# Attention and octonion feed-forward on one Trainium2 core: down weights expanded on GpSimd, one deviation for the second sequence's layer norm, gate products begun among the last scores, longer lags in the planner

## The chip, the core and the metric

The kernel runs on one NeuronCore of one Trainium2 chip. The time is that of the device, in microseconds, for one execution of the whole program, and the runs of the kernel before have a median of 1032.09 us. The core has a matrix engine (TensorE, PE in the profile; its weight loads are PEld), three other compute engines (VectorE or DVE, ScalarE or ACT, GpSimd or POOL), and a queue engine for transfers (SyncE or SP). Each runs its own list of instructions in order, and an instruction waits until the semaphores of what it needs have been raised. DMAs are issued from the lists of SP and POOL.

## The reference

The input x has 2 sequences of 1024 tokens of 512 values. Everything is float32.

```python
xn = (x - mean(x)) / sqrt(var(x) + eps)                      # per token
q, k, v = split(xn @ w_qkv.T + b_qkv)                        # 32 heads of 16
scores = q @ k.T / 4 + slope[head] * position[key]           # ALiBi, causal
s = (softmax(scores) @ v) @ w_out.T + b_out
Wq = clip(round(W / mean|W|), -1, 1) * mean|W|               # ternary weights
gate, up = oct(xn, w_gate), oct(xn, w_up)                    # 512 -> 1360
ffn = oct(silu(gate) * up, w_down)                           # 1360 -> 512
out = x + s * silu(ffn)
```

An `oct` layer treats its features as 8 components. Its full matrix consists of the 8 component matrices, each used 8 times with a sign from the octonion multiplication table. "Expanding" a weight means writing these signed copies out.

## The kernel before, in words

**Tiling.** Tokens lie on 16 tiles of 128. Attention is cut into 32 units (b, g, qc): a sequence, one of 8 groups of 4 heads, and one half of the queries (512 columns). Each unit is worked twice. The first pass makes scores (L566) only to find a maximum for each query: DVE reduces the banks (tiles `s` and `s_d`, written into `left` and `mx`), and `split_max` and `place_max` (L619, L631; small products `pm`) put the maxima into two rows of the query stack `q_stack`, with small GpSimd DMAs from `mr`. The second pass makes the scores with the maximum already subtracted (L682), adds the causal mask by a product (L701), ACT takes the exponential into `p` (128x512 at a time), and `p` times the values accumulates in `po` (L720), with the sums of the exponentials in extra rows.

**A unit's result.** `finish` (L733) yields six chores: `sums` fetches the sums with a DMA into `l`, `invert` takes the reciprocal on DVE, `keep` stores it to DRAM (`ld`), `spread` (L757) loads it into `r`, each head's row repeated on 32 partitions, `divide` (L765) multiplies `po`'s copy by `r` on DVE, and `store` writes the result to `att`, from which the output projection loads `oT` (products `pout`, L803). Each chore has a lag in ns, which the planner lets pass before it writes the next one.

**Side work among the scores.** Projections to queries and keys (`pqk`, L479), values (`pv`, L439), transposes of the normed tokens (`ptx`, L404) and the output projection are placed among the score products. So are the weights of the feed-forward part. For `w_down`, `expand_down` (L354) writes the signed copies for each of four parts kp into one buffer `m_d` with 8 activations on ACT, in two halves, and `turn_down` (L366) transposes them on PE (tile `ptd`), copies them with ACT to `md`, and stores them to DRAM (`mw`) with GpSimd DMAs. The buffer of `m_d` is single. `md` is in the ring of tag "ot", which has two buffers and also holds `r`.

**Second sequence.** Tokens 8 to 15 are normed during the score phase, by `more_tokens` (L975), in two groups of four: load four tiles, `measure` on DVE, `deviation` (a square root on ACT, which needs another function table than the exponential) and `factors`, `normal` on ACT, and the transposes.

**Order.** Until `held.clear()` (L1392) all compute and DMA-issuing instructions keep the order in which the Python code emits them on each engine (`InOrder`, L59). That order is written by a planner (L1107 to L1390) which counts its own time `now` and, for every engine, a time when it would be free (`run_pe`, `run_act`, `run_dve`). At each `step` it takes the next ready score product, or else value products, the small products for the maxima, and side work by due time (`next_side`, `next_behind`). `later` puts items in the list `behind` with a position at which they may begin and a model of their cost. `do_chores` emits the chores of finished units, `try_fill` the loads of `q_stack` and `k_stack`.

**Gate phase.** After the loop, the normed tokens are split into a part in the reduced format and a remainder (`split`, L1410: GpSimd makes `xh`, DVE makes `xl`). `expand_in` (L1429) writes gate and up weights of a 128-row tile from their signs, gate on ACT and up on DVE. `gate_up` (L1447) makes 8 products each for `pg` and `pu` (L1455), and `down` (L1476) accumulates the down projection (`pd`, L1497). The work goes over 4 blocks of 512 tokens and 11 hidden tiles. The last chunks of the output projection stand among them.

Of the kernel before, what the change touches and what calls it, by code (L numbers as in the profile page):

```python
# [10 lines left out]
F32 = mybir.dt.float32  # L11
# [7 lines left out]
P = 128  # L19
# [56 lines left out]
def kernel(  # L76
# [277 lines left out]
    def expand_down(kp, half):  # L354

        if half == 0:
            nat[kp] = wop.tile([P, 8, H8], F32, tag="wo", name=f"m_d_{kp}")
        for k in range(4 * half, 4 * half + 4):
            act_.activation(
                nat[kp][:, k, :],  # L360
                w_tiles["d"][:, k ^ kp * 2, :],
                AF.Identity,
                scale=sgn["d"][:, kp, k : k + 1],
            )

    def turn_down(kp, first):  # L366

        m = nat[kp].rearrange("p k o -> p (k o)")
        last = min(first + 4, NM)
        pt = ps_m.tile([P, 4, P], F32, tag="m", name=f"ptd_{kp}_{first}")  # L370
        for mt in range(first, last):
            fs = min(P, HID - mt * P)
            pe(nc.tensor.transpose(pt[:fs, mt - first, :], m[:, mt * P : mt * P + fs], ident))
        md = wk.tile([P, 4, P], F32R, tag="ot", name=f"md_{kp}_{first}")
        full = min(last, HID // P) - first
        act_.copy(md[:, 0:full, :], pt[:, 0:full, :])
        pool_.dma_start(
            out=mw[first : first + full, :, kp, :].rearrange("m p n -> p m n"),
            in_=md[:, 0:full, :].bitcast(F32),
        )  # L380
        if last == NM:
            fs = HID - (NM - 1) * P
            act_.copy(md[:fs, full, :], pt[:fs, full, :])
            pool_.dma_start(out=mw[NM - 1, 0:fs, kp, :], in_=md[:fs, full, :].bitcast(F32))
# [348 lines left out]
    def finish(b, g, qc):  # L733


        posb = po_tiles.pop((b, g, qc))
        key = f"{b}_{g}_{qc}"
        box = {}

        def sums():  # L740
            box["l"] = wk.tile([P, 16], F32, tag="l", name=f"l_{key}", bufs=1)
            sp_.dma_start(
                out=box["l"],
                in_=posb[HD:P:32, :].rearrange("h (a n) -> h a n", n=16),
            )

        def invert():
            box["rl"] = wk.tile([P, 16], F32, tag="rl", name=f"rl_{key}", bufs=1)
            dve_.reciprocal(box["rl"], box["l"])

        def keep():
            box["dram"] = spill.tile([4, 512], F32, tag="l", name=f"ld_{key}")
            sp_.dma_start(
                out=box["dram"].rearrange("h (a n) -> (h a) n", n=16), in_=box["rl"]
            )

        def spread():  # L757
            box["r"] = wk.tile([P, 512], F32, tag="ot", name=f"r_{key}")
            for h in range(4):
                sp_.dma_start(  # L760
                    out=box["r"][32 * h : 32 * h + 32],
                    in_=box["dram"][h : h + 1].to_broadcast([32, 512]),
                )

        def divide():  # L765
            dve_.tensor_tensor(box["r"], posb, box["r"], ALU.mult)

        def store():
            sp_.dma_start(out=att[b, g, :, qc * 512 : qc * 512 + 512], in_=box["r"])


        return [
            (sums, 0, 9000),
            (invert, 250, 300),
            (keep, 0, 3500),
            (spread, 0, 7000),
            (divide, 620, 300),
            (store, 0, 4500),
        ]

# [124 lines left out]
        return "weights" not in known  # L905

    def waits_x():
        return any(it[2] == "x" or it[2] and it[2][0] == "n" for it in behind)


    order = sorted(range(len(side)), key=lambda n: side[n][0])
# [55 lines left out]
    def spread(kp, half):  # L967
        later(
            lambda: expand_down(kp, half),
            lambda: set_known(  # L970
                ("e", kp), run_act(max(now[0], known["w", "d"]), 1300)
            ),
        )

    def more_tokens(t0):  # L975

        for t in range(t0, t0 + 4):
            later(
                lambda t=t: measure(t, 4),
                lambda t=t: set_known(("m", t), run_dve(max(now[0], known["x"]), 900)),  # L980
                "x",
            )
            begin[0] += 0.2
        later(
            lambda: (deviation(t0, 4), factors(t0, 4)),
            lambda: run_dve(run_act(known["m", t0 + 3], 2800), 350),
        )
        for t in range(t0, t0 + 4):
            begin[0] += 0.3
            later(  # L990
                lambda t=t: normal(t, 4),
                lambda t=t: set_known(("n", t), run_act(now[0], 720)),
            )
            later(lambda t=t: norm_item(t), None, ("n", t), 436, "t")

    def load_wo():
        wo_sb.append(wop.tile([P, KD, D], F32, tag="wo", name="wo_sb"))
# [94 lines left out]
        for f in range(0, NM, 4):  # L1092
            later(lambda kp=kp, f=f: turn_down(kp, f), None, ("e", kp), 436, "t")
    later(lambda: set_known("weights", 0))
    for t0 in (8, 12):
        begin[0] = 3 if t0 == 8 else 5.4
        later(
            lambda t0=t0: [load_x(t, sp_) for t in range(t0, t0 + 4)],
            lambda: set_known("x", now[0] + 9000),
        )  # L1100
        begin[0] += 0.4
        more_tokens(t0)
    begin[0] = 10
    later(load_wo)
    side = [(d, ok or (lambda: True), it) for d, ok, it in lead_in + side]
# [14 lines left out]
    RUN = 1800  # L1120
    HELD = 1e12
    now, kind = [HEAD], ["F"]
    act, dve = [0.0], [0.0]
    e_free, x_free, m_free = [0.0] * 2, [0.0] * 3, [0.0] * 2
    o_free = [0.0]
    p_ready, placed, fill_at = {}, {}, []
# [12 lines left out]
    def run_act(t, cost):  # L1139
        act[0] = max(act[0], t) + cost  # L1140
        return act[0]

    def run_dve(t, cost):
        dve[0] = max(dve[0], t) + cost
# [195 lines left out]
    def step():  # L1340
# [10 lines left out]
        if kind[0] == "R" and soon(scores):  # L1351
            scores[0][3]()
            return True
        rest = next_value() + next_turn() + next_side(pos) + next_behind(pos)
        rest.sort(key=lambda f: (max(f[0], now[0] + SOON), f[1]))
        if soon(rest) and (left[0] > 0 or not soon(scores)):
            left[0] -= rest[0][2]
# [20 lines left out]
            for m in range(2):  # L1378
                sp_.dma_start(out=swapped[:, :, m, :], in_=pairs[:, :, 1 - m, :])

    left = [RUN]
    while E[0] < len(exps) or V[0] < len(vals) or S_[0] < len(side) or behind:
        try_fill()
        do_chores()
        try_fetch()
        if not w_again and unit_of(exps, E[0]) >= NU - 5:
            fetch_signs()
        if not step():
            now[0] += 500
            assert now[0] < 1e8  # L1390

    held.clear()  # L1392


    fw = []
    for t in [
        k_ring[2],
        k_ring[3],
        k_ring[4],
        q_ring[3],  # L1400
        k_ring[1],
        q_ring[2],
        k_ring[0],
        vp.tile([P, 4, 3 * P], F32R, tag="v", name="fw_7"),
    ] + [pp.tile([P, 4, 512], F32R, tag="p", name=f"fw_{n}") for n in (8, 9, 10)]:
        t = t.rearrange("p h n -> p (h n)")[:, 0 : 12 * P]
        fw.append(t.rearrange("p (s n) -> p s n", n=P))
    halves, downs = {}, {}

    def split(tb):  # L1410
# [11 lines left out]
        dve_.tensor_tensor(xl, src, xh, ALU.subtract)  # L1422
        halves[tb] = (xh, xl)

    def load_fw(mt):
        fs = min(P, HID - mt * P)
        sp_.dma_start(out=fw[mt][:fs, 8:12, :].bitcast(F32), in_=mw[mt, 0:fs])

    def expand_in(mt):  # L1429

        fs = min(P, HID - mt * P)
        for n in range(2):
            for kt in range(KD):
                f = 0
                while f < fs:
                    k, o = divmod(mt * P + f, H8)
                    size = min(fs - f, H8 - o)
                    dst = fw[mt][:, 4 * n + kt, f : f + size]
                    src = w_again[n][:, k ^ kt * 2, o : o + size]
                    sign = sgn["i"][:, kt, k : k + 1]  # L1440
                    if n:
                        dve_.tensor_scalar_mul(dst, src, sign)
                    else:
                        act_.activation(dst, src, AF.Identity, scale=sign)
                    f += size

    def gate_up(tb, mt):  # L1447
        fs = min(P, HID - mt * P)
        pg = ps_x.tile([P, 512], F32, tag="x0", name=f"pg_{tb}_{mt}")
        pu = ps_x.tile([P, 512], F32, tag="x1", name=f"pu_{tb}_{mt}")  # L1450
        for n0, ps in ((0, pg), (4, pu)):
            for kt in range(KD):
                for n, part in enumerate(halves[tb]):
                    pe(
                        nc.tensor.matmul(  # L1455
                            ps[:fs, :],
                            lhsT=fw[mt][:, n0 + kt, 0:fs],
                            rhs=part[:, kt, :],
                            start=(kt == 0 and n == 0),
                            stop=(kt == KD - 1 and n == 1),  # L1460
                        )
                    )
        sg = wk.tile([P, 512], F32, tag="oT", name=f"sg_{tb}_{mt}")
        act_.activation(sg[:fs, :], pg[:fs, :], AF.Silu, scale=scale["g"][:fs, 0:1])
        h = wk.tile([P, 512], F32, tag="y", name=f"h_{tb}_{mt}")
# [78 lines left out]

    s_tiles = []
    fetch_last()
    split(0)
    for mt in range(2):
        expand_in(mt)
    for mt in range(NM):  # L1550
        load_fw(mt)

# [99 lines left out]
```

## Time and profile before

| | value |
|---|---|
| runs of the kernel before | 1032.09 us median (1031.54 to 1032.76) |
| profiled execution, its own time | 1030.97 us |
| its span | 1029.1 us |
| mean granted TensorE clock | 0.991 |
| PE busy | 988.5 us (96%) |
| DVE busy | 581.4 us (56%) |
| ACT busy | 490.6 us (48%) |
| POOL busy | 171.7 us (17%) |
| exponentials 128x512 | 576 at 596 ns |
| hardware queue of SP | 74384 packets, 111.40 MB, 35.1% of 16 engines |

The profile comes from one execution. Its page lists busy times, the granted clock, the DMA queues and the costliest groups of instructions; the trace behind it can be asked for the waits of an engine, for the busy time in stretches of the span, and for single instructions. A line such as "engine op out<-in shapes xcount | busy, mean" is a group of instructions, "L" is the line in the kernel (L69 is the helper that passes on every instruction except those of PE, so those are told apart by tile names). In a wait, the arrow names what ended it. In a line of the timeline, the first number is the start in us from the beginning of the span, the second the duration, and the brackets hold the idle time of the engine just before, with its releaser. DVE, ACT, POOL and SP being idle costs nothing by itself.

### The profile page before, as it was taken

How to read it: one execution, taken by the hardware profiler on the slowest of the kernel's cores; microseconds unless marked ns; L12 is line 12 of the kernel's file. 1: busy time of each engine (PE TensorE's matmuls, PEld its weight loads, DVE VectorE, ACT ScalarE, POOL GpSimd, SP SyncE). 2: the span in 40 equal slices, each digit the busy share in tenths (PEclk: the TensorE clock that was granted, in tenths of full speed). 3: DMA queues.
4: the chain of work that ended last, by engine and by line, in shares of the span. 5: the costliest groups of instructions: out<-in, count | busy, mean ns of one | idle time of the engine just before them, and what ended most of it. 6: DMA issues, size and time to landing. Idle time of an engine off the chain costs nothing. (4 is left out here: it accounts for less than half of the span.)

```text
span 1029.1 us, 15486 instructions
## 1 busy us (share of the span) xinstructions
PE 988.5 (96%) x5290; PEld 669.1 (65%) x5290; DVE 581.4 (56%) x1726; ACT 490.6 (48%) x942; POOL 171.7 (17%) x289
## 2 busy tenths in 40 slices
PE   8999988999999999899999999989999999999996
PEld 6655645775666676656667656545476678788784
DVE  6588945776577675676766757748251132231312
ACT  4034456756656554456654556556761132232322
POOL 7701023100200200010010000010021133232322
PEclk9999998999999999999999999999999999999998
DMA  5854735244454423433533244532242113030201
GB/s 203 244 150 154 169 129 167 63 131 154 144 150 138 137 66 123 152 109 117 166 95 96 84 130 148 124 100 79 86 148 82 51 66 109 1 123 1 94 29 42
DMA packets 77935, 117.16 MB, mean 114 GB/s; under 512 B 19624, under 2 KB 29488, under 8 KB 77856
## 3 DMA queue, kind: packets, MB, share of 16 engines
q1 hardware_dynamic: 74384, 111.40, 35.1%
q0 software_dynamic: 3424, 4.64, 1.6%
q8 instruction: 42, 0.69, 0.3%
q14 instruction: 37, 0.30, 0.1%
q10 hardware_dynamic: 48, 0.13, 0.0%
HBM read 77.77 MB, written 37.56 MB: 112 GB/s over the span
## 5 line engine op out<-in xcount | busy, mean ns | idle before, releaser
L69 ACT ACTIVATE p<-s 128x512 f32<-128x512 f32 x576 | 319.4, 596 | 183.4 <-PE s L701 105.7
L682 PE MATMUL s<-q_stack,k_stack 128*128 128x512 f32 (+3 forms) x768 | 263.0, 408 | 4.9 <-ACT p L69 4.5
L69 DVE TENSOR_REDUCE left<-s 128x1 f32<-128x512 f32 x256 | 161.4, 681 | 71.2 <-PE s L566 70.9
L682 PEld LDWEIGHTS s<-q_stack,k_stack 128*128 128x128 f32 x768 | 132.4, 191 | 88.3 <-ACT p L69 44.2
L69 DVE CUSTOM_DVE_ANT_0 nowhere<-s_d,mask 128x384 uint8<-128x384 f32 (+2 forms) x384 | 139.6, 419 | 21.4 <-PE s_d L566 20.0
L720 PE MATMUL po<-p,v 128*32 128x512 f32 (+3 forms) x1536 | 142.6, 491 | 2.8 <-ACT p L69 2.8
L566 PE MATMUL s_d<-k_stack,q_stack 126*128 126x384 f32 (+3 forms) x512 | 128.5, 348 | 4.0 <-DVE mx L69 3.6
L479 PE MATMUL pqk<-xnT,wq 128*128 128x512 f32 x256 | 128.3, 601 | 3.2 <-ACT md L69 1.2
L69 POOL DMA_DIRECT2D q_stack<-mr x64 | 31.0, 488 | 558.5 <-ACT mr L69 558.5
L69 DVE SCALAR_TENSOR_TENSOR h<-pu,sc_u,sg 128x512 f32<-128x512 f32 (+1 forms) x44 | 33.0, 750 | 152.2 <-PE pu L1455 146.7
L566 PEld LDWEIGHTS s_d<-k_stack,q_stack 126*128 126x128 f32 x512 | 83.4, 192 | 26.4 <-DVE mx L69 11.2
L69 DVE CUSTOM_DVE_ANT_0 s_d<-s_d,mask 128x512 f32<-128x512 f32 x128 | 85.6, 715 | 21.9 <-PE s_d L566 21.6
L566 PE MATMUL s<-k_stack,q_stack 126*128 126x512 f32 x256 | 86.5, 422 | 7.9 <-DMA q_stack<-sp 5.7
L69 POOL TENSOR_TENSOR hs<-h,hs 128x512 fp32r<-128x512 f32 (+1 forms) x43 | 56.2, 1307 | 211.6 <-ACT hs L69 211.6
L720 PEld LDWEIGHTS po<-p,v 128*32 128x32 f32 x1536 | 43.4, 109 | 72.6 <-issue 57.9
L701 PE MATMUL s<-mask_r,ident_r 128*128 128x256 f32 (+1 forms) x320 | 89.7, 280 | 0.0
L69 ACT ACTIVATE sg<-pg,sc_g 128x512 f32<-128x512 f32 (+1 forms) x44 | 30.2, 687 | 104.4 <-PE pg L1455 104.4
L69 ACT CAST hs<-h 128x512 fp32r<-128x512 f32 (+1 forms) x44 | 27.3, 620 | 84.4 <-DVE h L69 84.4
L439 PE MATMUL pv<-wv,xnT 128*128 128x256 f32 x256 | 65.1, 384 | 0.0
L701 PEld LDWEIGHTS s<-mask_r,ident_r 128*128 128x128 f32 x320 | 61.1, 191 | 2.8 <-issue 1.7
L566 PEld LDWEIGHTS s<-k_stack,q_stack 126*128 126x128 f32 x256 | 47.1, 190 | 23.6 <-issue 5.8
L479 PEld LDWEIGHTS pqk<-xnT,wq 128*128 128x128 f32 x256 | 44.5, 190 | 27.2 <-issue 18.6
(149 smaller groups left out, 1152.0 us busy)
## 6 DMA issues: line engine op xcount, KB each, us to landing
sp<-st SPq DMA_DIRECT2D x32, 512.0 KB
k_stack<-sp SPq DMA_DIRECT2D x128, 128.0 KB
q_stack<-sp SPq DMA_DIRECT2D x128, 128.0 KB
wqr<-in_wqk_dram SPq DMA_DIRECT2D x16, 512.0 KB
r<-ld SPq DMA_DIRECT2D x128, 64.0 KB
att<-r SPq DMA_DIRECT2D x32, 256.0 KB
xt<-in_x_dram SPq DMA_DIRECT2D x16, 256.0 KB
oT<-att SPq DMA_DIRECT2D x32, 128.0 KB
```

The source lines that it names most:

```text
L69: ins = issue(*args, **kwargs)
L439: nc.tensor.matmul(ps[:, 0:256], lhsT=xnT[:, c, b * S + kt * P : b * S + (kt + 1) * P], rhs=wv_tiles[2 * b + hh][:, c, :], start=(c == 0), ...
L479: nc.tensor.matmul(ps, lhsT=wq_tiles[b, gp][:, kt, which, :], rhs=xnT[:, kt, b * S + c * 512 : b * S + (c + 1) * 512], start=(kt == 0), st ...
L566: nc.tensor.matmul(ps, lhsT=q_of(b, g, qc)[0 : NR - 2, h, tl * P : (tl + 1) * P], rhs=k_of(b, g, c)[0 : NR - 2, h, :n], start=True, stop=True,
L682: nc.tensor.matmul(ps[:, c0 : c0 + w], lhsT=k_of(b, g, kt // 4)[0:NR, h, kt % 4 * P : (kt % 4 + 1) * P], rhs=q[0:NR, h, 512 - w : 512], st ...
L701: pe(nc.tensor.matmul(out, lhsT=ident_r, rhs=rhs, start=False, stop=True))
L720: nc.tensor.matmul(po[32 * i : 32 * i + 32, 512 - w : 512], lhsT=v[:, kt, h * VC : h * VC + 32], rhs=p[:, i * part + c0 : i * part + c0 + ...
```

## The change

The diff does five things.

1. `expand_down` runs on GpSimd instead of ACT (32 multiplies of 128x170), and the planner counts a time for GpSimd (`gps`, `run_pool`). `md` moves from the ring "ot" to the ring "oT".
2. `spread` issues one DMA instead of four, whose source repeats each of the 4 rows 32 times. The lags after `invert`, `spread` and `divide` grow from 300 to 2000, 7000 to 8000 and 300 to 2500 ns.
3. For the second sequence, all eight token tiles are measured first; there is one `deviation` and one `factors`. Tokens 12 to 15 are normed next, then tokens 8 to 11 are loaded a second time and normed. `waits_x` covers the three loads.
4. When the exponentials have reached the last unit but one and all maxima are placed, `try_ahead` splits the first block and expands gate and up weights of hidden tiles 0 and 1, on GpSimd and DVE. It then offers 24 gate and up products of the first block (`pg_0`, `pu_0` and `pg_1`, the last in the bank "x2") to the planner through `next_ahead`. What is not taken is emitted after the loop.
5. As a result of 4, `expand_in`, `split` and the buffers `fw` move ahead of the loop, and `gate_up` uses the products that have been begun.

The number of instructions on PE is the same. ACT has 898 instead of 945 instructions, POOL 335 instead of 291, SP 606 instead of 698.

```diff
     def expand_down(kp, half):
...
-            act_.activation(
-                nat[kp][:, k, :],
-                w_tiles["d"][:, k ^ kp * 2, :],
-                AF.Identity,
-                scale=sgn["d"][:, kp, k : k + 1],
+            pool_.tensor_scalar_mul(
+                nat[kp][:, k, :], w_tiles["d"][:, k ^ kp * 2, :], sgn["d"][:, kp, k : k + 1]
             )
...
-        md = wk.tile([P, 4, P], F32R, tag="ot", name=f"md_{kp}_{first}")
+        md = wk.tile([P, 4, P], F32R, tag="oT", name=f"md_{kp}_{first}")
...
         def spread():
             box["r"] = wk.tile([P, 512], F32, tag="ot", name=f"r_{key}")
-            for h in range(4):
-                sp_.dma_start(
-                    out=box["r"][32 * h : 32 * h + 32],
-                    in_=box["dram"][h : h + 1].to_broadcast([32, 512]),
-                )
+            sp_.dma_start(
+                out=box["r"],
+                in_=box["dram"].rearrange("h (e n) -> h e n", e=1).to_broadcast([4, 32, 512]),
+            )
...
             (sums, 0, 9000),
-            (invert, 250, 300),
+            (invert, 250, 2000),
             (keep, 0, 3500),
-            (spread, 0, 7000),
-            (divide, 620, 300),
+            (spread, 0, 8000),
+            (divide, 620, 2500),
             (store, 0, 4500),
...
     def waits_x():
-        return any(it[2] == "x" or it[2] and it[2][0] == "n" for it in behind)
+        return any(it[2] and it[2][0] in "xn" for it in behind)
...
             lambda: set_known(
-                ("e", kp), run_act(max(now[0], known["w", "d"]), 1300)
+                ("e", kp), run_pool(max(now[0], known["w", "d"]), 1500)
             ),
...
+    def more_tokens():
+
+        begin[0] = 3
+        load_tokens(8, "x")
+        begin[0] += 0.4
+        measure_tokens(8, "x")
+        load_tokens(12, "x2")
+        begin[0] += 0.4
+        measure_tokens(12, "x2")
+        later(
+            lambda: (deviation(8, 8), factors(8, 8)),
+            lambda: run_dve(run_act(now[0], 2800), 350),
+            ("m", 15),
+        )
+        normal_tokens(12, "x2")
+        load_tokens(8, "x3")
+        begin[0] += 0.4
+        normal_tokens(8, "x3")
...
-        rest = next_value() + next_turn() + next_side(pos) + next_behind(pos)
+        rest = next_value() + next_turn() + next_side(pos) + next_behind(pos) + next_ahead()
...
-    def expand_in(mt):
+    def expand_in(mt, parts=(0, 1), beside=False):
...
-                    if n:
-                        dve_.tensor_scalar_mul(dst, src, sign)
+                    if n or beside:
+                        eng = pool_ if beside and n != mt else dve_
+                        eng.tensor_scalar_mul(dst, src, sign)
                     else:
                         act_.activation(dst, src, AF.Identity, scale=sign)
...
+    def try_ahead():
+        if ahead_at[0] < HELD or M[0] < len(maxs) or len(placed) < NU:
+            return
+        if unit_of(exps, E[0]) < NU - 2:
+            return
+        expand_in(0, (0,), True)
+        split(0)
+        expand_in(0, (1,), True)
+        expand_in(1, (0, 1), True)
+        ahead_at[0] = run_dve(now[0], 6500)
+        run_dve(now[0], 2500)
+        for mt, n in ((0, 0), (0, 1), (1, 0)):
+            begun[mt, n], products = gate_or_up(0, mt, n)
+            ahead.extend(products)
+
+    def next_ahead():
+        if not ahead:
+            return []
+
+        def go():
+            ahead.pop(0)()
+            run_pe("R", ready, 227)
+
+        ready = ahead_at[0]
+        return [(ready, 8, 0, go)]
...
-    split(0)
-    for mt in range(2):
-        expand_in(mt)
+    while ahead:
+        ahead.pop(0)()
     for mt in range(NM):
         load_fw(mt)
```

More of the change, by code (lines that the diff above doesn't have):

```diff
@@ L970, in spread, with load_tokens, measure_tokens, normal_tokens @@
             lambda: set_known(
-                ("e", kp), run_act(max(now[0], known["w", "d"]), 1300)
+                ("e", kp), run_pool(max(now[0], known["w", "d"]), 1500)
             ),
         )
-    def more_tokens(t0):
+    def load_tokens(t0, key):
+        later(
+            lambda: [load_x(t, sp_) for t in range(t0, t0 + 4)],
+            lambda: set_known(key, now[0] + 9000),
+        )
+    def measure_tokens(t0, key):
         for t in range(t0, t0 + 4):
             later(
-                lambda t=t: measure(t, 4),
-                lambda t=t: set_known(("m", t), run_dve(max(now[0], known["x"]), 900)),
-                "x",
+                lambda t=t: measure(t, 8),
+                lambda t=t: set_known(("m", t), run_dve(max(now[0], known[key]), 900)),
+                key,
             )
             begin[0] += 0.2
[L984 to L987, printed above, removed]
+    def normal_tokens(t0, key):
         for t in range(t0, t0 + 4):
@@ L990, in more_tokens @@
             later(
-                lambda t=t: normal(t, 4),
-                lambda t=t: set_known(("n", t), run_act(now[0], 720)),
+                lambda t=t: normal(t, 8),
+                lambda t=t: set_known(("n", t), run_act(max(now[0], known[key]), 720)),
+                key,
             )
             later(lambda t=t: norm_item(t), None, ("n", t), 436, "t")
+    def more_tokens():
[6 more added lines that the diff above has]
+        measure_tokens(12, "x2")
+        later(
+            lambda: (deviation(8, 8), factors(8, 8)),
+            lambda: run_dve(run_act(now[0], 2800), 350),
+            ("m", 15),
+        )
+        normal_tokens(12, "x2")
+        load_tokens(8, "x3")
+        begin[0] += 0.4
+        normal_tokens(8, "x3")
     def load_wo():
@@ L1094 @@
     later(lambda: set_known("weights", 0))
[L1095 to L1102, printed above, removed]
+    more_tokens()
     begin[0] = 10
@@ L1122 @@
     now, kind = [HEAD], ["F"]
-    act, dve = [0.0], [0.0]
+    act, dve, gps = [0.0], [0.0], [0.0]
     e_free, x_free, m_free = [0.0] * 2, [0.0] * 3, [0.0] * 2
@@ L1141, in run_act, with run_pool @@
         return act[0]
+    def run_pool(t, cost):
+        gps[0] = max(gps[0], t) + cost
+        return gps[0]
     def run_dve(t, cost):
@@ L1379, in fetch_signs, with add_fw @@
                 sp_.dma_start(out=swapped[:, :, m, :], in_=pairs[:, :, 1 - m, :])
[L1381 to L1392, printed above, removed]
-    fw = []
[L1396 to L1405, printed above, removed]
+    fw = []
+    def add_fw(t):
         t = t.rearrange("p h n -> p (h n)")[:, 0 : 12 * P]
         fw.append(t.rearrange("p (s n) -> p s n", n=P))
+    for t in (k_ring[2], k_ring[3], k_ring[4], q_ring[3], k_ring[1], q_ring[2], k_ring[0]):
+        add_fw(t)
     halves, downs = {}, {}
@@ L1423, in split @@
         halves[tb] = (xh, xl)
-    def load_fw(mt):
+    def expand_in(mt, parts=(0, 1), beside=False):
         fs = min(P, HID - mt * P)
-        sp_.dma_start(out=fw[mt][:fs, 8:12, :].bitcast(F32), in_=mw[mt, 0:fs])
-    def expand_in(mt):
-        fs = min(P, HID - mt * P)
-        for n in range(2):
+        for n in parts:
             for kt in range(KD):
@@ L1445, in expand_in, with gate_or_up, product @@
                     f += size
+    def gate_or_up(tb, mt, n):
+        fs = min(P, HID - mt * P)
+        tag, name = (("x0", "pg"), ("x1", "pu"))[n] if (tb, mt) != (0, 1) or n else ("x2", "pg")
+        ps = ps_x.tile([P, 512], F32, tag=tag, name=f"{name}_{tb}_{mt}")
+        def product(kt, i):
+            pe(
+                nc.tensor.matmul(
+                    ps[:fs, :],
+                    lhsT=fw[mt][:, 4 * n + kt, 0:fs],
+                    rhs=halves[tb][i][:, kt, :],
+                    start=(kt == 0 and i == 0),
+                    stop=(kt == KD - 1 and i == 1),
+                )
+            )
+        return ps, [lambda kt=kt, i=i: product(kt, i) for kt in range(KD) for i in range(2)]
@@ new lines @@
+    ahead, ahead_at, begun = [], [HELD], {}
+    def try_ahead():
[12 more added lines that the diff above has]
+            ahead.extend(products)
@@ new lines, in next_ahead @@
+    def next_ahead():
[6 more added lines that the diff above has]
+        return [(ready, 8, 0, go)]
+    left = [RUN]
+    while E[0] < len(exps) or V[0] < len(vals) or S_[0] < len(side) or behind:
+        try_fill()
+        do_chores()
+        try_fetch()
+        if not w_again and unit_of(exps, E[0]) >= NU - 5:
+            fetch_signs()
+        try_ahead()
+        if not step():
+            now[0] += 500
+            assert now[0] < 1e8
@@ L1447, in gate_up, with load_fw @@
+    held.clear()
+    for t in [vp.tile([P, 4, 3 * P], F32R, tag="v", name="fw_7")] + [
+        pp.tile([P, 4, 512], F32R, tag="p", name=f"fw_{n}") for n in (8, 9, 10)
+    ]:
+        add_fw(t)
+    def load_fw(mt):
+        fs = min(P, HID - mt * P)
+        sp_.dma_start(out=fw[mt][:fs, 8:12, :].bitcast(F32), in_=mw[mt, 0:fs])
     def gate_up(tb, mt):
         fs = min(P, HID - mt * P)
-        pg = ps_x.tile([P, 512], F32, tag="x0", name=f"pg_{tb}_{mt}")
-        pu = ps_x.tile([P, 512], F32, tag="x1", name=f"pu_{tb}_{mt}")
@@ L1451, in gate_up @@
[L1451 to L1462, printed above, removed]
+        both = []
@@ L1463, in gate_up @@
+        for n in range(2):
+            if tb == 0 and (mt, n) in begun:
+                ps = begun.pop((mt, n))
+            else:
+                ps, products = gate_or_up(tb, mt, n)
+                for emit in products:
+                    emit()
+            both.append(ps)
+        pg, pu = both
         sg = wk.tile([P, 512], F32, tag="oT", name=f"sg_{tb}_{mt}")
```

## The prediction

> **What bounds the kernel now.** I read the page's busy shares first, then the windows of the stages that the diff touches, then TensorE's waits, then the timeline at each wait. The shares say who sets the time:
>
> ```profile
> PE 988.5 (96%) x5290; PEld 669.1 (65%) x5290; DVE 581.4 (56%) x1726; ACT 490.6 (48%) x942; POOL 171.7 (17%) x289
> ```
>
> TensorE (PE) is busy for 988.5 of 1029.1 us. The change takes no product away from it, so only its 40.6 us of idle time, and time in which it runs at a lower clock, can be won. The windows (columns PE, PEld, DVE, ACT, POOL, then the granted clock, DMA share and GB/s) show where that lies:
>
> ```profile
> 120.00:150.00 30.00, 24.79 (x101) 13.15 (x93) 17.98 (x34) 15.57 (x38) 6.29 (x10) 0.94 0.45 140
> 150.00:180.00 30.00, 25.23 (x142) 16.71 (x142) 16.60 (x72) 18.52 (x46) 9.98 (x22) 0.89 0.49 155
> 180.00:240.00 60.00, 60.00 (x374) 42.37 (x373) 42.52 (x129) 38.50 (x69) 4.84 (x7) 1.00 0.34 104
> 718.00:750.00 32.00, 30.49 (x180) 15.41 (x181) 9.02 (x39) 23.80 (x61) 0.96 (x2) 1.00 0.30 99
> ```
>
> From 120 to 180 us, where the down weights are expanded and turned, PE is idle for 10.0 of 60 us and its clock falls; from 180 us on it is never idle, at 1.00. The seam to the gate phase (718 to 750) loses 1.5 us by the window. PE's waits (total, times, longest) name the rest:
>
> ```profile
> PE s L566 <- DMA q_stack<-sp: 5.7, 3, 3.4
> PE s L682 <- ACT p L69: 4.5, 7, 1.5
> PE s_d L566 <- DVE mx L69: 3.6, 5, 2.7
> PE po L720 <- ACT p L69: 2.8, 2, 2.2
> PE s L566 <- DVE left L69: 2.2, 1, 2.2
> ```
>
> The timeline says what is late behind these names (start, duration, then in brackets the idle time before and its releaser). First the 120 to 180 stage:
>
> ```profile
> 136.53 0.58 ACT L69 CAST md<-ptd 128x512 fp32r<-128x512 f32 x1 [3.28 <-DMA mw<-md]
> 137.17 0.70 PE L479 MATMUL pqk<-xnT,wq 128*128 128x512 f32 x1 [1.20 <-ACT md L69]
> 155.76 0.50 PE L682 MATMUL s<-q_stack,k_stack 128*128 128x512 f32 x1 [1.46 <-ACT p L69]
> 166.49 0.62 PE L720 MATMUL po<-p,v 128*32 128x512 f32 x1 [2.21 <-ACT p L69]
> ```
>
> ACT, in its written order, stands 3.28 us at a copy whose buffer is not yet stored; exps queue behind it, and PE waits for those exps or for the bank. Then the divisions and one fill:
>
> ```profile
> 95.11 0.69 DVE L69 TENSOR_TENSOR r<-posb,r 128x512 f32<-128x512 f32 x1 [2.73 <-DMA r<-ld]
> 96.46 0.50 PE L566 MATMUL s<-k_stack,q_stack 126*128 126x512 f32 x1 [2.20 <-DVE left L69]
> 423.49 0.69 DVE L69 TENSOR_TENSOR r<-posb,r 128x512 f32<-128x512 f32 x1 [4.13 <-DMA r<-ld]
> 424.90 0.44 PE L566 MATMUL s_d<-k_stack,q_stack 126*128 126x384 f32 x1 [2.66 <-DVE mx L69]
> 684.25 0.96 PE L566 MATMUL s<-k_stack,q_stack 126*128 126x512 f32 x3 [3.39 <-DMA q_stack<-sp]
> ```
>
> DVE waits for the reciprocal sums (`r`), and PE a moment later for a reduce queued behind that division. At 684 a query fill was issued late: SP stood 8 us at the store of a divided result.
>
> **(a) Down weights on GpSimd.** Gone from ACT are 32 activations:
>
> ```profile
> L69 ACT ACTIVATE m_d<-w_d,sgn_d 128x170 f32<-128x170 f32 x32 | 10.9, 428 | 3.8 <-DVE w_d L69 3.8
> L69 POOL COPY wq<-wqr 128x128 f32<-128x128 f32 x64 | 15.6, 293 | 17.2 <-issue 11.9 <-PE pqk L479 5.2
> L69 POOL TENSOR_SCALAR xt<-xt,rs,nb 128x512 f32<-128x512 f32 x2 | 1.5, 766 | 6.5 <-DVE rs L69 3.9 <-DVE nb L69 2.6
> ```
>
> No row has a GpSimd multiply of 128x170. Between 293 ns for 128 columns and 766 for 512, it is 293 + 473 x 42/384 = 345 ns; 32 make 11.0 us, on an engine that is busy for 16.3 us of these 60. So ACT's 10.9 us leave and GpSimd has room. At stake are 10.0 us of PE's idle time plus the slow clock: 24.79 x 0.06 + 25.23 x 0.11 = 4.3 us of PE work, 14.3 in all. The copies also move to the ring "oT", away from `r`; they may still wait for their own stores (256 KB land 2.9 us after issue).
>
> What speaks against it is GpSimd's own queue. The stores of a turned part are issued there too (707 ns each), and the one buffer of expanded weights is free for part kp+1 only when PE has transposed the last of part kp. So between the last transposes of kp and the first of kp+1 stand two copies (0.37 + 0.26 us), two store issues (1.41) and 4 to 8 expansions (1.4 to 2.8): 3.5 to 4.8 us. In the new order PE has some 40 products there before part 1 and some 12 with a value group (5 us) before part 3, but only five maximum products and a small transpose (1.25 us) before part 2: a new wait of about 3 us. I keep 5 of the 14.3 us lost (this wait, and about 2 for clock and copies): **gain 9**. Ends: 14 if all is covered; below nothing if the gaps at all three parts are uncovered, 3 x 4.2 = 12.6 against 14.3, and each expansion is slower than 345 ns.
>
> [...] DVE is busy for 34.6 of these 60 us. By the row the 32 multiplies take 11.0 us. [...]
>
> **(b) Reciprocal sums.** Four issues per unit become one (96 fewer of SP's), and the division comes 2.7 us later in the planner's time: lags before it are 9000 + 300 + 3500 + 7000 = 19.8 us, then 9000 + 2000 + 3500 + 8000 = 22.5. Before, PE lost 2.20 + 2.66 and 0.56 us (three short waits at 296 to 298) = 5.4 us, for 11.1 us of DVE waiting at `r`. [...] The main queue's 35.1% of 16 engines over 74,384 packets is 77.7 ns a packet of 1.5 KB, so about 106 ns for 2 KB (estimate). [...] The last piece leaves SP 1.3 us earlier (1.82 us of issue at 416.87, about 0.5 after, as one fill of 128 KB takes). [...] Gain between 2.7 and 4.5: **3.5**.
>
> **(c) Fills.** In the new order the key and query fills stand ahead of the store and the load that held SP before 684. Of 3.39 us I take **3**; ends 0 and 3.4.
>
> **(d) Seam.** The splits, the expansion of the first gate tiles (12 of the multiplies now GpSimd's) and 24 gate products move to before the loop's end, 11 of them ahead of the last value products. A gate product is 227 ns; at 718, 723 to 726 and 749 PE waited 1.14 + 0.51 + 0.19 + 0.20 + 0.57 = 2.6 us for maxima and exps. Fillers cover most: **2**. The two copies to half precision (1.9 us of GpSimd, about 3 of DVE) and the multiplies lie beside the last exps, where DVE has 9 of 32 us of work; uncovered, they would cost 5 us.
>
> **(e) Layer norm.** One deviation instead of two removes two table loads of 1.28 us and one wait for the statistics from ACT; PE waited for neither pair. Four tokens are loaded twice, 4 x 256 KB where the DMA share is 0.34. **0.2**, ends 0 and 2.6 (if the exps behind were late).
>
> **Sum.** 9 + 3.5 + 3 + 2 + 0.2 = 17.7 us against the profiled 1030.97. The planner's new costs reorder nearly every engine from about 95 us on; waits of the kind removed (19 us in PE's five longest rows, over some 900 us) will return somewhere. I take back 3.5, a fifth. 1030.97 - 17.7 + 3.5 = 1016.8; the median of the runs shown is 1.1 above the profiled run, so **1018**.
>
> **Rivals.** *GpSimd becomes the bound of the 110 to 180 stage* (20%): for it, the single buffer and the shared ports; against it, 16 of 60 us busy. Gain (a) is lost: 1018 + 9 = 1027, down to 1033 if PE waits 5 us at each part.
> *Slower: the single load of `r`* (12%). [...] PE lost 5.4 us for 11.1 of DVE's wait, so 0.49 a us. Without (b) the kernel stands at 1021.5; 10.6 us more bring it back to 1032.1, which needs 22 us of DVE wait, 0.7 in each of 32 units. At 1 us each: 1037. [...] Against: 27 of 32 loads were in time before.
> *The stalls only move* (6%): the 19 us of waits return entirely, 1030 to 1034, no change. For it: order differs throughout. Against: the stage at 120 to 180 is limited by work that really leaves.
>
> **How the numbers follow.** 62% for 1018 (own range 1010 to 1025: ends of a, c and the reordering), 20% for 1027, 12% for 1037, 6% for 1032. The range 1007 to 1033 leaves out most of the slow rival and a sliver below. A change under 0.2% (2 us) can't be told from none: faster 62 + 17 + 1 = 0.80, same 3 + 2 = 0.05, slower 12 + 3 = 0.15.
>
> **What would show it.** (a) 120 to 180 with PE at 56 us or more and the clock at 0.97 or above; transposes waiting for GpSimd's `m_d` a few us in all. (b) DVE's wait for `r` below 5 us. (c) No query fill of 3 us near 680. (d) Gate products among the last exps, under 1 us of waits. (e) Five table loads. I am wrong if PE's waits name GpSimd or `r` for over 10 us, or if the stage at 120 to 180 keeps 10 us of idle time.

## The result and the profile after

The changed kernel takes 1036.97 us (median of 20 runs, 1032.49 to 1044.12) against 1031.96 us (20 runs, 1029.4 to 1035.44) for the kernel before. The ratio is 1.0052, with a 95% interval of 1.0038 to 1.0066: half a per cent slower, where 1018 us and a faster kernel had been forecast. The profiled execution of the changed kernel took 1038.6 us, its span is 1036.8 us and its mean granted clock 0.984 (before: 1030.97, 1029.1 and 0.991). Span times the missing share of the clock is 16.6 us after and 9.3 before.

TensorE's share in the page of the changed kernel looks like before:

```profile
PE 992.8 (96%) x5290; PEld 666.8 (64%) x5290; DVE 582.9 (56%) x1724; ACT 476.4 (46%) x895; POOL 203.5 (20%) x333
```

ACT has lost 14 us of work and GpSimd has gained 32. What the waits of the changed kernel name (total, times, longest) has changed:

```profile
PE s_d L563 <- DVE mx L69: 6.4, 4, 2.7
PE s L679 <- ACT p L69: 4.0, 6, 2.0
PE s L563 <- DVE left L69: 3.6, 3, 1.3
PE pu L1450 <- DVE h L69: 2.7, 2, 2.5
PE s_d L563 <- DVE left L69: 2.6, 1, 2.6
PE ptd L370 <- POOL m_d L69: 1.7, 6, 0.5
...
PE s L563 <- DMA q_stack<-sp: 1.7, 1, 1.7
```

The waits for exps and fills became shorter, those for DVE longer. DVE's own waits hold the reason:

```profile
DVE r L69 <- DMA r<-ld: 28.6, 11, 5.9
```

DVE stands 28.6 us at the division, in 11 of the 32 units. In the kernel before it stood 11.1 us, in 5:

```profile
DVE r L69 <- DMA r<-ld: 11.1, 5, 4.1
```

The windows of the changed kernel (columns as in the prediction) show what came of each stage:

```profile
120.00:150.00 30.00, 28.79 (x168) 17.43 (x168) 24.17 (x62) 17.61 (x35) 15.05 (x22) 1.00 0.50 147
150.00:180.00 30.00, 24.84 (x126) 16.19 (x125) 17.49 (x58) 14.03 (x29) 16.91 (x31) 0.84 0.45 137
180.00:240.00 60.00, 56.69 (x343) 39.31 (x341) 41.72 (x128) 32.80 (x59) 11.05 (x15) 0.99 0.44 137
718.00:750.00 32.00, 31.29 (x156) 16.06 (x158) 11.09 (x42) 24.01 (x58) 11.02 (x15) 0.89 0.29 94
290.00:300.00 10.00, 7.45 (x32) 3.59 (x33) 5.64 (x22) 2.16 (x5) 0.98 (x2) 0.83 0.40 118
763.00:770.00 7.00, 6.93 (x23) 5.54 (x24) 0.93 (x3) 4.29 (x13) 4.11 (x3) 0.76 0.36 111
```

In the first 30 us TensorE has 4 us more work than before; then the stage lasts longer, with TensorE's last waits behind it at 188 and 192 us. The two last rows lie behind waits for `r`. The timeline shows those chains (start, duration, in brackets the idle time before and its releaser):

```profile
285.57 0.55 SPq L69 DMA_DIRECT2D r<-ld  x1
291.14 0.69 DVE L69 TENSOR_TENSOR r<-posb,r 128x512 f32<-128x512 f32 x1 [2.66 <-DMA r<-ld]
292.55 0.44 PE L563 MATMUL s_d<-k_stack,q_stack 126*128 126x384 f32 x1 [2.56 <-DVE mx L69]
...
754.71 0.55 SPq L69 DMA_DIRECT2D r<-ld  x1
761.66 0.69 DVE L69 TENSOR_TENSOR r<-posb,r 128x512 f32<-128x512 f32 x1 [5.13 <-DMA r<-ld]
763.07 0.50 PE L1450 MATMUL pu<-q_stack,k_stack 128*128 128x512 f32 x1 [2.54 <-DVE h L69]
```

The single load of `r` leaves SP in 0.55 us, and the divisions that wait for it start 5.6 and 7.0 us after its issue began. DVE's list is in order, so the masked maximum behind the division is late, and TensorE loses 2.56 us; from 290 to 300 us it gets 0.83 of its clock. The same happens in the gate phase, where nothing of the kind stood before.

Where the time went can be followed by the moments at which TensorE has done equal amounts of work in both traces (each product counted by a fixed time for its kind). At 209 us of the kernel before, the changed one is 5.2 us ahead, at 276 us 6.4, at 300 us about 1; at 344 us it is about 1 behind, at 546 us 3.4, at 707 us 0.6, at 776 us 5.5. The large steps downward, 276 to 300 and 756 to 776, hold the two chains above.

### The profile page after: what moved, and what is told of

The parts are those of the page before. It is cut to its first block, busy times and chain, and to the rows that moved or that the text cites. A ratio compares the mean times of both kernels' runs of the same rounds, so it can differ in the third digit from the quotient of the medians.

```text
span 1036.8 us, 15321 instructions
## 1 busy us (share of the span) xinstructions
PE 992.8 (96%) x5290; PEld 666.8 (64%) x5290; DVE 582.9 (56%) x1724; ACT 476.4 (46%) x895; POOL 203.5 (20%) x333
## 5 line engine op out<-in xcount | busy, mean ns | idle before, releaser
L679 PE MATMUL s<-q_stack,k_stack 128*128 128x512 f32 (+3 forms) x768 | 266.0, 412 | 4.3 <-ACT p L69 4.0
L563 PE MATMUL s_d<-k_stack,q_stack 126*128 126x384 f32 (+3 forms) x512 | 126.4, 342 | 9.5 <-DVE mx L69 6.4
L563 PE MATMUL s<-k_stack,q_stack 126*128 126x512 f32 x256 | 89.2, 423 | 8.2 <-DVE left L69 3.6
```

What stands on the lines that cost most here:

```text
L563: nc.tensor.matmul(ps, lhsT=q_of(b, g, qc)[0 : NR - 2, h, tl * P : (tl + 1) * P], rhs=k_of(b, g, c)[0 : NR - 2, h, :n], start=True, stop=True,
L679: nc.tensor.matmul(ps[:, c0 : c0 + w], lhsT=k_of(b, g, kt // 4)[0:NR, h, kt % 4 * P : (kt % 4 + 1) * P], rhs=q[0:NR, h, 512 - w : 512], st ...
```

## The experiments

All kernels were timed beside the kernel before on the same chip. The experiments ran on four chips, on which the kernel before had medians from 1031.21 to 1031.96 us, so their ratios compare better than their times. Theory 1 was that the single load is carried by few DMA engines and lands late; the rival was that the longer lags let the chains of two units collide at the single buffers of `l` and `rl`.

**One load or four, in the changed kernel.** The planner does not see the number of loads, so the order of all other instructions is the same.

```diff
-            sp_.dma_start(
-                out=box["r"],
-                in_=box["dram"].rearrange("h (e n) -> h e n", e=1).to_broadcast([4, 32, 512]),
-            )
+            for h in range(4):
+                sp_.dma_start(
+                    out=box["r"][32 * h : 32 * h + 32],
+                    in_=box["dram"][h : h + 1].to_broadcast([32, 512]),
+                )
```

> The changed kernel with the load of r issued as four pieces again; the order of everything else is as in the changed kernel. Theory 1 (the single load is carried by few DMA engines and lands late): from issue to division it took 5.1 to 7.0 us in the changed kernel where DVE waited, and 3.6 to 4.3 in the kernel before, so each of DVE's 11 waits for r shrinks by about 1.9 us, from 28.6 us in all to about 10; PE gets back some 9 us and clock: 1027 us. Theory 2 (the longer lags and the single buffers of l and rl make the chains of two units collide): DVE still waits over 20 us for r, and SP has 96 more issues: 1036 to 1039.

Measured: 1022.08 us (1021.27 to 1024.28), ratio 0.9905 (0.9888 to 0.9921). The single load alone costs 15 us here, more than the 10 that Theory 1 expected, and all the rest of the change is a gain of about 10. Its row in DVE's waits:

```profile
DVE r L69 <- DMA r<-ld: 5.4, 5, 1.8
```

**Two loads of two heads each.** If the number of issues decides, this kernel has to lie between the other two.

```diff
+            for h in range(0, 4, 2):
+                sp_.dma_start(
+                    out=box["r"][32 * h : 32 * h + 64],
+                    in_=box["dram"][h : h + 2]
+                    .rearrange("h (e n) -> h e n", e=1)
+                    .to_broadcast([2, 32, 512]),
+                )
```

> The changed kernel with the load of r as two pieces of two heads each. [...] If only the number of issues or the size of one transfer matters, this kernel lies between one piece and four: 1030 to 1036.

Measured: 1062.45 us (1060.47 to 1063.27), ratio 1.0288 (1.0269 to 1.0308), outside the 1030 to 1036 that go with the number of issues or the size of a transfer, and 25.5 us above the single load.

```profile
DVE r L69 <- DMA r<-ld: 61.3, 17, 6.2
```

Two loads are far worse than one, and one is worse than four: neither the number of issues nor the bytes, which are the same in all three, can order them so. From the beginning of the issue to the division, over those units in which DVE stood waiting, the median is 3.9 us with four loads, 5.6 with one and 8.7 with two.

The records of the packets show another difference. A load of `r` is 128 packets of 2 KB, and where no other packets of this size are about, one can count how many are under way at once: with one load (near 768 us) exactly four for 2.2 of 3.1 us, with two (near 294) exactly two for 5.4 of 6.0. With four loads, issued one after the other (near 523), it is mostly five to eight and at most eleven, and all have passed in 1.9 us. A single packet takes about the same in all three, 92, 96 and 93 ns in the mean. Four at a time, 128 packets are 32 one behind another, two at a time 64; from one load to two the division comes 3.2 us later, 0.10 us for each of the 32 more. So the order of the three kernels is that of the packets under way at once. The profile does not name the engine of a packet: that few engines carry a load, as Theory 1 has it, was not shown, nor why these loads differ so.

**The single load in the kernel before**, with the old lags:

```diff
-            for h in range(4):
-                sp_.dma_start(
...
+            sp_.dma_start(
+                out=box["r"],
+                in_=box["dram"].rearrange("h (e n) -> h e n", e=1).to_broadcast([4, 32, 512]),
+            )
```

> The kernel before with the single load of r alone; lags and order as before. Theory 1: each load lands 1.9 us later, and the old lags leave less room than the new: DVE waits for r 25 us or more instead of 11, and the kernel takes 1038 to 1045 us. Theory 2 (the lags and the collisions are the cause): the same as before within 2 us.

Measured: 1044.2 us (1042.4 to 1046.78), ratio 1.0116 (1.0095 to 1.0136), 12 us slower.

```profile
DVE r L69 <- DMA r<-ld: 30.5, 11, 5.8
```

The rival of the lags is not needed for the loss: no lag was changed here.

**Down weights on GpSimd alone**, in the kernel before: the activations of `expand_down`, the ring of `md`, and the planner's cost, as in the change.

```diff
-            act_.activation(
...
-                scale=sgn["d"][:, kp, k : k + 1],
+            pool_.tensor_scalar_mul(
+                nat[kp][:, k, :], w_tiles["d"][:, k ^ kp * 2, :], sgn["d"][:, kp, k : k + 1]
             )
...
-        md = wk.tile([P, 4, P], F32R, tag="ot", name=f"md_{kp}_{first}")
+        md = wk.tile([P, 4, P], F32R, tag="oT", name=f"md_{kp}_{first}")
...
-                ("e", kp), run_act(max(now[0], known["w", "d"]), 1300)
+                ("e", kp), run_pool(max(now[0], known["w", "d"]), 1500)
```

> The kernel before with part (a) alone: down weights expanded on GpSimd, md in the ring oT, the planner's cost for GpSimd. If the gain of the four-piece kernel in its 110 to 210 us stretch (7 us ahead of the kernel before at the same amount of TensorE work) comes from part (a): 1023 to 1027 us, although one multiply takes 718 ns there instead of the 345 of my sum. If it came from the lags or the layer norm: 1030 to 1034.

Measured: 1020.04 us (1017.84 to 1022.13), ratio 0.9882 (0.9861 to 0.9903). Part (a) alone is worth 12 us, more than the 5 to 9 expected.

**The two halves of that, each alone.** First the ring:

```diff
-        md = wk.tile([P, 4, P], F32R, tag="ot", name=f"md_{kp}_{first}")
+        md = wk.tile([P, 4, P], F32R, tag="oT", name=f"md_{kp}_{first}")
```

> The kernel before with one letter changed: md in the ring oT instead of ot; expansion stays on ACT. If the gain credited to GpSimd (part a alone: 1020.0 us) comes from md no longer standing behind r in a ring of two: 1018 to 1023 us. If it comes from taking 10.9 us of activations off ACT: 1028 to 1032.

Measured: 1029.29 us (22 runs, 1026.54 to 1033.78), ratio 0.9979 (0.9968 to 0.9991), about 2 us. Then GpSimd with `md` left in "ot":

> The kernel before with the down weights expanded on GpSimd, md left in the ring ot. If the ring is the cause: 1030 to 1036 us, since GpSimd's 718 ns multiplies only add to the chain. If the engine is the cause: 1019 to 1024.

Measured: 1024.11 us (1021.49 to 1025.04), ratio 0.9921 (0.9904 to 0.9937), 8 us. So the engine is the larger half, and the ring does not explain most of it. The 12 us of both together are not told from the sum of the two.

**The longer lags alone**, in the kernel before:

```diff
-            (invert, 250, 300),
+            (invert, 250, 2000),
...
-            (spread, 0, 7000),
-            (divide, 620, 300),
+            (spread, 0, 8000),
+            (divide, 620, 2500),
```

> The kernel before with the longer lags alone (2000, 8000 and 2500 ns), four loads of r. By part (b) of the sum without the single load: DVE's wait for r falls from 11 us to 4 to 6, and the time by 2 to 4 us: 1028 to 1030. If the longer lags mostly let the chains of two units collide at the single buffers of l and rl (waits of 6.7 us in the four-piece kernel): 1031 to 1034.

Measured: 1027.15 us (1025.24 to 1030.17), ratio 0.9953 (0.9937 to 0.997), a gain of almost 5 us, a little more than the 2 to 4 expected. DVE's wait for `r` falls to 2.8 us, while the reciprocal's wait for the store of the unit before grows from 1.4 to 3.3.

**The four-load kernel with the expansion on ACT again**, `md` in "oT":

```diff
-            pool_.tensor_scalar_mul(
-                nat[kp][:, k, :], w_tiles["d"][:, k ^ kp * 2, :], sgn["d"][:, kp, k : k + 1]
+            act_.activation(
...
+                scale=sgn["d"][:, kp, k : k + 1],
             )
...
-                ("e", kp), run_pool(max(now[0], known["w", "d"]), 1500)
+                ("e", kp), run_act(max(now[0], known["w", "d"]), 1300)
```

> The four-piece kernel (1022.1 us) with the down weights expanded on ACT again, md in the ring oT. If part (a) is worth what it seems in the trace: 1027 to 1031, with TensorE's waits for exps in 120 to 180 us back. If the gain came from moving md to another ring: within 2 us of the four-piece kernel.

Measured: 1018.97 us (1016.2 to 1020.56), ratio 0.9869 (0.9848 to 0.989). Both expectations missed: ACT is here about 3 us better than GpSimd, whose part was worth 8 us in the other order (the two intervals against the kernel before just touch). One candidate stands in the trace of the four-load kernel, where GpSimd still has the work:

```profile
L69 POOL TENSOR_SCALAR m_d<-w_d,sgn_d 128x170 f32<-128x170 f32 x32 | 22.5, 715 | 5.1 <-DVE w_d L69 5.0
```

```profile
186.12 1.27 POOL L69 DMA_DIRECT2D mw<-md  x2 [2.02 <-ACT md L69]
187.38 2.04 POOL L69 MEMSET v<- 128x2304 f32 x1
...
189.46 0.43 DVE L69 TENSOR_TENSOR v<-pv,bv_sb 128x256 f32<-128x256 f32 x1 [4.93 <-POOL v L69]
...
190.53 0.50 PE L563 MATMUL s_d<-k_stack,q_stack 126*128 126x384 f32 x2 [2.58 <-DVE left L69]
```

The multiply takes 715 ns there. The clearing of the value tile `v` is behind the last expansion and its stores on GpSimd; DVE waits 4.93 us for it, and TensorE 2.58 behind DVE. Yet the kernel with ACT has a DVE wait of 7.8 us for `v` as well, and TensorE waits 2.4 us shortly before it ends. So this wait does not account for the difference, whose cause stays open.

**The four-load kernel without products ahead:** `try_ahead` is not called, and after the loop the splits and the expansions stand as before.

```diff
-        try_ahead()
...
-    while ahead:
-        ahead.pop(0)()
+    split(0)
+    for mt in range(2):
+        expand_in(mt)
```

> The four-piece kernel (1022.1 us) without part (d): splits and expansions after the loop as in the kernel before, no gate products among the last scores. By my sum the part is worth 2 us: 1023 to 1025. If it is worth nothing, because the waits before it (1.2 us for the last maxima and exps) stay and the products were never needed as fillers: 1021 to 1023.

Measured: 1024.64 us (1023.57 to 1029.36), ratio 0.9932 (0.9907 to 0.9958), 2.5 us more than with them. The intervals overlap, so the 2 us of the sum are likely, not shown.

**Two buffers for `l`.** The kernel with four loads and ACT, with the reciprocal taken in place, so that two buffers fit in the old space:

```diff
-            box["l"] = wk.tile([P, 16], F32, tag="l", name=f"l_{key}", bufs=1)
+            box["l"] = wk.tile([P, 16], F32, tag="l", name=f"l_{key}")
...
-            box["rl"] = wk.tile([P, 16], F32, tag="rl", name=f"rl_{key}", bufs=1)
+            box["rl"] = box["l"]
```

> The kernel with four loads and the expansion on ACT (1019.0 us), the reciprocal taken in place in l, which then has two buffers in the same space. If the reciprocal's waits for the store of the unit before it (5.0 us of DVE for ld<-rl, 2.7 for another load) cost TensorE about half: 1015 to 1018. If they are covered: within 1.5 us of 1019.

Measured: 1017.37 us (4 runs, 1014.82 to 1020.07), ratio 0.9862 (0.9841 to 0.9883). The waits of the reciprocal are gone from the list, but against the 1018.97 us this is not told from nothing.

**The layer norm as before**, in the four-load kernel (GpSimd), and in the last kernel (ACT, two buffers of `l`): `more_tokens`, its two calls and `waits_x` are those of the kernel before.

```diff
-    more_tokens()
+    for t0 in (8, 12):
+        begin[0] = 3 if t0 == 8 else 5.4
+        later(
+            lambda t0=t0: [load_x(t, sp_) for t in range(t0, t0 + 4)],
+            lambda: set_known("x", now[0] + 9000),
+        )
+        begin[0] += 0.4
+        more_tokens(t0)
```

> The four-piece kernel (1022.1 us) with the second sequence's layer norm as in the kernel before: two deviations, four table loads in the score phase, no second load of tokens 8 to 11. If part (e) is worth what the sum says (0.2 us, at most 2.6): 1022 to 1025. If the new order of the layer norm costs time (the parts alone, GpSimd with the ring 12 us and the lags 5, add up to more than the four-piece kernel has): 1015 to 1020.

Measured: 1023.93 us (1021.16 to 1026.69), ratio 0.9919 (0.9906 to 0.9933): not told from the 1022.08 with the new layer norm.

> The kernel with four loads, the expansion on ACT, ring oT and two buffers of l (1017.4 us), with the layer norm as in the kernel before. If the new layer norm costs time of itself: 1011 to 1015. If it costs only where GpSimd's expansion stands beside it, or nothing: 1016 to 1020.

Measured: 1011.6 us (4 runs, 1009.83 to 1012.49), ratio 0.9806 (0.9793 to 0.982). Without the new layer norm this one is 6 us faster. It beats both kernels, by 1.9 and by 2.4 per cent. Its windows beside those above:

```profile
120.00:150.00 30.00, 27.99 (x137) 16.45 (x135) 24.30 (x61) 19.09 (x45) 7.23 (x16) 1.00 0.49 155
150.00:180.00 30.00, 25.57 (x161) 17.89 (x161) 15.55 (x55) 19.32 (x47) 10.90 (x15) 0.89 0.56 167
180.00:240.00 60.00, 59.40 (x341) 39.53 (x341) 41.10 (x125) 39.64 (x69) 1.92 (x4) 1.00 0.35 111
```

The down-weight stage still loses 6.4 us of 60; GpSimd is free of the expansion and TensorE is nearly full after 180 us.

## Why the prediction was wrong, point by point

**The step that failed is (b),** "gain between 2.7 and 4.5: 3.5". It has two halves. The longer lags alone gain almost 5 us in the kernel before; the single load costs 15 us in the changed kernel, and 12 in the kernel before. The 3.5 us rest on a lateness of 1.25 us, the author's estimate, which no run shows; measured, it is 1.9 (the division 5.6 us after issue in the median, 3.7 before). That is the smaller error.

The larger one is the overlap: the lateness was set against all 2.7 us of added lag, from the sums to the division. Of these, 1.7 stand ahead of `keep`, and only 1.0 between the load and the division. And a lag is the planner's time, not the room that DVE leaves. By a lag of 8 us, a load that can be used 5.6 us after its issue would never be late. But in the trace of the four-load kernel, with TensorE's order as in the changed kernel, DVE was ready for the division less than 5.6 us after the issue began in 12 of 32 units, and less than 3 us in three of them. These are the units in which a load of 5.6 us is late; with the single load, 11 were. Both ends of (b) were gains, although a slower rival stood in the text; with its 1037 as one end the range would have held the result.

**The rival that ended slower was right in its cause,** DVE's wait for the single load (28.6 us, and 5.4 with four loads). Its size, 1037 worked out and 1036.97 measured, is in part luck, because two errors cancelled. It took 32 us of DVE's wait at 0.49 us of the kernel's time for each. The single load raises the wait by 23.2 us and the time by 14.9 (0.64), in the kernel before by 19.4 and 12.2 (0.63), two loads by 55.9 and 40.4 (0.72). The 0.49 counted TensorE's idle time alone and left out the lower clock behind it. Nor did the wait come as 0.7 or 1 us in each of 32 units: 11 units waited 2.6 us each.

**(a)** "Gain 9" is near to what the part does alone in the kernel before (12), but not for the reasons given, and in the order of the changed kernel it was no gain: with four loads, the expansion on ACT is about 3 us faster than on GpSimd, in intervals that just touch. The multiply was taken from between two rows of other operations as 345 ns and measures 718 in the mean, so the 32 take 22.6 us and not 11; the rival that GpSimd becomes the bound deserved more than 20%. That rival also names shared ports, which no run shows; the durations are even (703 to 929 ns, median 708). Why a 128x170 multiply takes almost as long as the 766 ns of 128x512 stays open. In the changed kernel TensorE's waits for `m_d` are only 1.7 us, but the stage is stretched to 192 us: 53.6 us of work in 60, where 56 were to show it right. The ring alone, counted at nothing, gives 2 us.

**(c)** The wait of 3.39 us at 684 became 1.16, which is 2.2 of the 3 us taken, but not as argued. The query fill left SP no earlier, first before, then in the changed kernel:

```profile
678.96 2.59 SPq L69 DMA_DIRECT2D q_stack<-sp  x4
...
679.49 2.54 SPq L69 DMA_DIRECT2D q_stack<-sp  x4
```

TensorE came to it later (683.9 us, before 680.9). The profile names the store `att<-r` as what ended the wait, but that store was issued behind the fill, at 682.1. The wait at this place is 3.56 us with part (a) alone and 0.53 with the lags alone, so its shortening goes with the lags.

**(d)** The 2 us are in line with 2.5 measured without certainty, but the seam keeps 1.24 us of waits, and a stretch at half speed follows (a clock of 0.57 from 720 to 728 us). **(e)** Five table loads, as said. Its 0.2 us hide a reordering: nothing in one kernel, 6 us of cost in another.

The 3.5 us taken back for reordering were a guess, and a fifth was too little: (a) and the lags alone give 12 and 5 us, and everything but the single load together gives 10. So with four loads the kernel takes 1022 us, near the forecast of 1018, but its parts were not what the forecast had.

## What to carry to other kernels

Four transfers into one were no saving here, where the one load had four packets under way at a time and the four had mostly five to eight: look at how many packets of each shape are under way at once, and compare the time from issue to use with the room between exactly these two in the trace, not with the planned lag of the whole chain. Leave a loss as an end for every unmeasured term. Undo one part at a time before a mixed change is judged: here one line hid 15 us, and what GpSimd's part and the new layer norm are worth depended on the parts around them.

## What the runs showed that was not expected

In both traces TensorE's granted clock falls to 0.50 in pieces of 3.4 us or twice that, apart from the end of the span: four of 3.4 in the kernel before, four of 3.4 and two of 6.8 in the changed one. In the changed kernel this happens, among others, after the waits of 2 to 3 us at 292, 428 and 763 us, and at 720 after three short ones of 1.24 us in all. The window at the seam is the clearest:

```profile
720.00:728.00 8.00, 7.93 (x26) 3.02 (x27) 3.90 (x10) 3.73 (x7) 8.00 (x10) 0.57 0.32 101
```

TensorE is almost never idle there (busy for 7.93 us), and loses 3.4 of 8 us.

Not every wait is followed by it. In the kernel before, the waits of 2.20 us at 96 and of 3.39 us at 684 left the clock at 1.00, while after the one of 2.66 us at 425 it fell (the clock is the third number from the end):

```profile
94.00:104.00 10.00, 7.80 (x42) 4.42 (x41) 6.97 (x12) 4.49 (x8) 0.00 (x0) 1.00 0.25 68
422.00:432.00 10.00, 7.34 (x44) 5.93 (x46) 7.06 (x31) 3.92 (x7) 0.00 (x0) 0.83 0.38 121
682.00:692.00 10.00, 7.75 (x35) 4.73 (x35) 6.54 (x12) 4.82 (x11) 1.89 (x1) 1.00 0.11 26
```

What decides between them was not found. Over the span the clock takes 9.3 us before, 16.6 in the changed kernel, 11.2 with four loads and 26.5 with two. So a wait of 2.5 us can cost 4 or more (an estimate: the wait and half of 3.4 us), which a sum over idle times does not show. Of the 14.9 us of the single load, some 5.4 are clock, by one profile of each kernel.
